# Attention and 64 experts on one core: the order of a product's seven steps with P7 ahead of P3, two places for ys, another place for the second expert's w2, and the first two experts alone

## The chip, the core and the metric

The kernel runs on one core of a Trainium2 chip. The time is device microseconds of one execution, from start to end on that core; lower is better. The engines have their own instruction streams and meet through semaphores: TensorE (PE in the profile, its weight loads PEld), VectorE (DVE), ScalarE (ACT), GpSimd (POOL) and SyncE (SP). Transfers are started by an instruction on a queue (here SP and POOL) and land later. The execution from which the profile was taken took 2610.53 us; the runs without a profile took 2606.79, 2606.75 and 2600.74, median 2606.75.

## The reference

The input x has 4 batches of 1024 rows and 1024 columns, all in float32. With xn the layer norm of x, the result is x + attention(xn) + experts(xn):

```python
q, v, gate = xn @ Wq, xn @ Wv, silu(xn @ Wg)          # each 4096 x 1024 by 1024 x 1024
states[s] = lam * states[s-1] + v[s]                   # a scan over the rows of a batch
y = layernorm(q * states) * ln_g + ln_b
attention = (y * gate) @ Wo                            # a fourth 1024 x 1024 product

# 64 experts over the 4096 rows: 8 per row (softmax, top 8), the first 128 rows of each expert count
h = silu(xg @ w1[e].T) * (xg @ v1[e].T)                # 128 x 1024 by 1024 x 384, twice
y = h @ w2[e]                                          # 128 x 384 by 384 x 1024
out[row of the slot] += y * weight of the slot
```

(The experts take the rows in the order (row, batch); the kernel gathers them by index.)

## The kernel before, in words

**Products in seven steps.** Each 1024-deep product of the attention (v, q, gate, Wo) is cut into 2 x 2 blocks and made with seven block products in place of eight (Strassen's, in Winograd's form). The function `steps` (L128) is a generator: each `next` issues one of the seven, always 8 matmuls of 128 x 512, and the small work behind it. Three PSUM banks are used: a takes P1 (B11), then P6 (T2), P7 (T3) and P4 (T4) added on top; b takes P2 (B21); c takes P5 (T1), then P3 (B22) on top. ACT copies a after P1, c after P5 and a after P6 into a scratch tile (`copied`, L153 to L156), and DVE adds these to a bank to give c11, c12 and c22 (L167, L176, L179). The last step ends with c21 in bank a, which the function `then` takes. Before the change the steps run P1, P2, P5, P6, P3, P7, P4. P7 reads and writes a, c22's add (L179) must read a after P7 and before P4 adds to it; c12's add (L176) reads c after P3.

`product` (L183) drives seven steps for v, q and gate in the first stage, with the last step of one product put between two steps of the next. The first stage, about 1226 us, goes over the 4 batches: layer norm and turn of x, routing (top 8 per row, first 128 rows per expert), the three products, the scan, the second norm (`find_spread`), and the gated rows written to DRAM.

**The experts.** From about 1226 us the class `Experts` runs the 64 experts with the Wo products in between. Each expert has three parts on PE: `hidden` (L943; the two products with w1 and v as one set of block products with seven in place of eight, its right-hand sums made by DVE in `right_sum`, L928, in place in the weight tiles and in t2, t3, t4; 9.08 us), `turn_hidden` (L999; three transposes into bank D, and ACT's copy to hT) and `output` (L1005; two times six matmuls with w2 into banks D and T, ACT's copy times the slot's weight into ys, L1014, and a scatter of ys with addition into the output, L1015, on GpSimd's queue; 5.2 us on PE).

The list `plan` in `run` says which experts go together, and how many Wo steps are put in: ahead of the group's first turn, between each turn and its output, and behind the group. A usual pair runs hidden, hidden, turn, one step, output, turn, two steps, output, and every other pair has one step behind it. Before, expert 0 is alone, then come the pairs (1, 2) to (61, 62), and 63 is alone. There are 16 units of Wo (`project`, L1034), 112 steps in all. The row half lo of a unit (olo) is added to the output by a DMA on GpSimd's queue when five steps have been issued, the other (ohi) in `then`, after the seventh. All these DMAs add into the same output tensor, and those that might touch the same rows as a scatter wait for it, and it for them.

**Order.** In the expert stage the instructions of PE, DVE and ACT are kept in program order (`in_order`, L86); those on SP and POOL are placed by the scheduler of the framework by their readiness. Places in SBUF are handed out by pools: `scratch` (4 tiles of 2 KB a partition) for ACT's copies and two small tiles of the routing, `line` (5 tiles of 4 KB), `left`, `quarter`, `three` and others.

**Loads.** `load(e, n)` (L830) brings v (n = 1), w1 (n = 0) or w2 (n = 2) of expert e, 1536 KB each, on SP's queue; v and w1 have two places each (by e odd or even), w2 has one place, and is loaded as two halves of columns. v and w1 of expert e + 2 are loaded when `hidden(e)` has been issued, w2 of e + 1 when `output(e)` has. `gather` (L850) brings an expert's 128 rows in four indirect DMAs on POOL (xg) and, in a fifth, the weights of its slots (wt, eight places).

Of the kernel before, what the change touches and what calls it, by code (L numbers as in the profile page):

```python
# [8 lines left out]
F32 = mybir.dt.float32  # L9
# [7 lines left out]
P = 128  # L17
# [24 lines left out]
NSLOT = 7  # L42
NWT = 8

# [60 lines left out]
class Pools:  # L105


    def __init__(self, ctx, tc):
        def pool(name, bufs, space=None):
            kw = {} if space is None else {"space": space}  # L110
            return ctx.enter_context(tc.tile_pool(name=name, bufs=bufs, **kw))

        self.one = pool("one", 1)
        self.three = pool("three", 3)
        self.quarter = pool("quarter", 9)
        self.left = pool("left", 2)
        self.line = pool("line", 5)
        self.scratch = pool("scratch", 4)
        self.small = pool("small", 2)

        self.ps2 = pool("ps2", 2, PSUM)
        self.ps1 = pool("ps1", 1, PSUM)
# [14 lines left out]
def steps(nc, pools, lhs, blocks, c11, c12, c22, then, name, begun=None):  # L137
# [28 lines left out]
    yield  # L166
    nc.vector.tensor_tensor(c11, b, s1, ALU.add)  # L167
    c = pools.bank("c", [P, SH], f"pc_{name}")
    acc(c, 4, "T1", True, True)
    s5 = copied(c, 5)  # L170
    yield
    acc(a, 5, "T2", False, True)
    s2 = copied(a, 2)
    yield
    acc(c, 6, "B22", False, True)
    nc.vector.tensor_tensor(c12, c, s2, ALU.add)  # L176
    yield
    acc(a, 3, "T3", False, True)
    nc.vector.tensor_tensor(c22, a, s5, ALU.add)  # L179
    yield  # L180
# [59 lines left out]
def attn_and_routing(  # L240
# [3 lines left out]
    nc = tc.nc  # L244
    one, line, scratch, small = pools.one, pools.line, pools.scratch, pools.small

# [228 lines left out]
    def scored(b):  # L475
# [4 lines left out]
        for k in reversed(range(KD)):  # L480
            for h in (1, 0):
# [7 lines left out]
                )  # L489
        both = scratch.tile([P, SH], F32, tag="sc", name=f"lgs_{b}")  # L490
        nc.scalar.copy(both, two)
# [9 lines left out]
    def route(b, lg):  # L501
# [5 lines left out]
        nc.vector.tensor_reduce(mx, lg, AX.X, ALU.max)  # L507
        sh = scratch.tile(wide, F32, tag="sc", name=f"sh_{b}")
        nc.vector.tensor_tensor(sh, lg, mx.unsqueeze(2).to_broadcast(wide), ALU.subtract)
# [311 lines left out]
class Experts:  # L821
# [8 lines left out]
    def load(self, e, n):  # L830


        if e >= E:
            return
        pools, (w, k) = self.pools, self.ws[n]
        slot = (n, e % 2) if n < 2 else (0, e % 2 ^ 1) if e == E - 1 else n
        if slot not in self.slots:
            t = (pools.x if e == 0 and n < 2 else pools.y)(f"w{n}_{e}")
            self.slots[slot] = t.rearrange("p a b -> p (a b)")
        t = self.weights[e, n] = self.slots[slot].rearrange("p (k f) -> p k f", k=k)  # L840
        if n == 2:
            from_ = w[e].rearrange("p (k f) -> p k f", k=k)
            for cols in (H0, H1):
                self.nc.sync.dma_start(out=t[:, :, cols], in_=from_[:, :, cols])
            return
        done = self.nc.sync.dma_start(out=self.slots[slot], in_=w[e])
        if (e, n) == (1, 1):
            self.tc.keep_in_program_order(done)

    def gather(self, e):  # L850
# [6 lines left out]
        for r in range(NQ):  # L857
# [5 lines left out]
            )  # L863
        nc.gpsimd.indirect_dma_start(
            out=self.wt[:, e % NWT, :],
            out_offset=None,
            in_=self.wtab,
            in_offset=bass.IndirectOffsetOnAxis(ap=self.idx[:, e : e + 1], axis=0),
        )

    def places(self):
# [9 lines left out]
        )  # L881
        self.p6, self.q = t[:, 2 * n : 2 * n + F], u[:, n : n + F]
        self.s = {0: pools.one.tile([P, 4, KH, TH], F32, tag="cur", name="s")}

    def more_places(self):

        pools = self.pools
        t = pools.line.tile([P, S], F32, tag="line", name="s1")
        self.s[1] = t.rearrange("p (i k c) -> p i k c", i=4, k=KH)
        self.ys = pools.line.tile([P, D], F32, tag="line", name="ys")  # L890
        t, u = (pools.scratch.tile([P, SH], F32, tag="sc", name=n) for n in ("act1", "up"))
        self.acts[1], self.up = t[:, 0:F], u[:, 0:F]

# [111 lines left out]
    def output(self, e):  # L1005
        nc, ys, hT = self.nc, self.ys, self.hT
        w2, wt = self.weights.pop((e, 2)), self.wt[:, e % NWT, e : e + 1]
        for h, cols in enumerate((H0, H1)):
# [11 lines left out]
            compute_op=ALU.add,  # L1020
        )


# [10 lines left out]
    def project(self, u, t):  # L1034
# [5 lines left out]

        def add(o, h):
            r0 = b * S + h * SH + m * P
            nc.gpsimd.dma_start(out=self.out[r0 : r0 + P, :], in_=o, accum_op=ALU.add)

        def then(c21):
            nc.scalar.copy(hi[:, H0], c21)
            add(hi, 1)

        for n, _ in enumerate(
            steps(nc, pools, t, self.wo_b, lo[:, H0], lo[:, H1], hi[:, H1], then, f"o_{u}")  # L1050
        ):
            if n == 4:
                add(lo, 0)
            yield

    def begin(self, idx, part):
        self.idx, self.part = idx, part
        v = self.pools.line.tile([P, S], F32, tag="line", name="act")
        self.acts = {0: v[:, 0:F]}
        self.hT = v[:, F : 2 * F].rearrange("p (j i) -> p j i", i=P)  # L1060
        self.wt = self.pools.small.tile([P, NWT, E], F32, tag="sel", bufs=1, name="wt")
        for n in (1, 0):
# [10 lines left out]
    def run(self):  # L1073
# [14 lines left out]

        last = E - 1
        plan = [((0,), 2, (1,), 0), ((1, 2), 0, (1, 2), 1)]  # L1090
        plan += [((e, e + 1), 0, (1, 2), e // 2 % 2) for e in range(3, last - 4, 2)]
        plan += [((e, e + 1), 0, (1, 1), 0) for e in (last - 4, last - 2)]
        plan += [((last,), 1, (0,), 0)]
        todo, u, left = None, 0, 0
# [12 lines left out]
        with in_order(self.tc, ORDERED):  # L1107
# [4 lines left out]
            self.more_places()  # L1112
            for group, ahead, between, behind in plan:
                new = group[-1] + 1
                for e in group:
                    self.hidden(e, e + 2 if e else 1, e != group[-1])
                    for n in (1, 0):
                        self.load(e + 2, n)
                    if e == last - 1:
                        self.load(last, 2)  # L1120
                    if e == group[0]:
                        self.gather(e + 4 if e else 3)
                project(ahead)
                for i, e in enumerate(group):
                    self.turn_hidden(e)
                    project(between[i])
                    if i == 0:
                        if e == 0:
                            for _ in wo_sums:
                                pass  # L1130
                            self.turned(2)
                        for n in (0, 1):
                            self.left_sums(new + n)
                        for n in (3, 1):
                            self.right_sum(new, n)
                    self.output(e)
                    if e + 1 < last:
                        self.load(e + 1, 2)
                    if i == 0:
                        self.gather(group[-1] + 4)  # L1140
                    if e == group[-1]:
                        for n in (2, 4):
                            self.right_sum(new, n)
# [51 lines left out]
```

## Time and profile before

| | before |
|---|---|
| median of 3 runs | 2606.75 us (2600.74 to 2606.79) |
| profiled execution, its time | 2610.53 us |
| its span | 2608.6 us |
| mean granted TensorE clock | 0.998 |
| first stage (0 to 1226 us) | PE busy 1218.06, DVE 796.30, DMA share 0.46 |
| expert stage (1226 to 2592 us) | PE busy 1332.03, DVE 908.82, ACT 366.06, POOL 508.60, DMA share 0.89 |
| HBM read, written | 483.67 MB, 124.81 MB |
| DMA packets | 164338, 593.25 MB |

A line of the waits reads: engine, operation's tile and its line, what it waited for, then us in total, times and longest. A line of the timeline reads: start and duration in us, engine, line, instruction, out<-in, tile and operand shapes, the count of instructions in the row, and in brackets the idle time before it and what ended that. The line numbers are those of the code above. The tail from 2592 us on holds the last two steps of the last Wo unit, the scatter of expert 63 and the last olo and ohi.

### The profile page before, as it was taken

What the parts mean: (1) busy time and instruction counts of PE and PEld (TensorE: products, weight loads), DVE (VectorE), ACT (ScalarE), POOL (GpSimd) and SP (SyncE); (2) the same over time, 40 slices, a digit from 0 to 9 for tenths busy, and PEclk for the clock granted to TensorE, in tenths of its full rate; (3) what the DMA queues carried; (4) which work ended last, traced back from release to release, by engine and by line L of the source; (5) the groups of instructions that cost most, each with busy time, mean ns of one, the idle gap of its engine ahead of it and who ended that gap; (6) DMA issues with size and microseconds to landing.
All of it is one profiled execution on the core that took longest, in us unless ns stands there. A gap on an engine that the chain in (4) does not pass through costs nothing. (4 is left out here: it accounts for less than half of the span.)

```text
span 2608.6 us, 23232 instructions
## 1 busy us (share of the span) xinstructions
PE 2557.6 (98%) x8453; PEld 1129.9 (43%) x8453; DVE 1705.8 (65%) x2116; ACT 612.7 (23%) x1048; POOL 777.6 (30%) x630
## 2 busy tenths in 40 slices
PE   9999999999999999999999999999999999999998
PEld 5444444444444444444444444444444444444443
DVE  7946686384954677266775767575767666666663
ACT  4113112131112211121222223222222222222322
POOL 1452302111021111222343434342434243334321
PEclk9999999999999999999999999999999999999999
DMA  5655625453245441336898988898889889898995
GB/s 188 252 185 207 188 93 165 181 152 119 106 136 214 146 144 67 139 105 231 290 320 281 309 284 311 285 329 269 294 295 319 291 284 300 291 295 289 309 296 138
DMA packets 164338, 593.25 MB, mean 227 GB/s; under 512 B 16880, under 2 KB 53744, under 8 KB 139392
## 3 DMA queue, kind: packets, MB, share of 16 engines
q1 hardware_dynamic: 123472, 448.04, 47.4%
q0 software_dynamic: 40320, 143.72, 20.9%
q8 instruction: 67, 1.10, 0.2%
q14 instruction: 47, 0.39, 0.0%
q10 hardware_dynamic: 432, 0.01, 0.0%
HBM read 483.67 MB, written 124.81 MB: 233 GB/s over the span
## 5 line engine op out<-in xcount | busy, mean ns | idle before, releaser
L940 DVE TENSOR_TENSOR t<-w 128x1536 f32<-128x1536 f32 x128 | 224.0, 1750 | 288.3 <-PE hC L958 285.5
L858 POOL DMA_INDIRECT xg<-rows,tables x256 | 308.0, 1203 | 298.7 <-DVE xgT L901 224.9
L1015 POOL DMA_INDIRECT out_dram<-ys,tables x64 | 117.5, 1836 | 434.7 <-ACT ys L1014 179.2
L144 PE MATMUL pa_g<-xT,w 128*128 128x512 f32 x512 | 230.8, 593 | 0.0
L144 PE MATMUL pa_q<-xT,w 128*128 128x512 f32 x480 | 216.6, 593 | 4.0 <-DVE y L179 4.0
L144 PE MATMUL pa_v<-xT,w 128*128 128x512 f32 x480 | 215.8, 592 | 0.0
L144 PE MATMUL pa_o<-wo_T,gated 128*128 128x512 f32 x384 | 174.2, 596 | 11.8 <-DVE ohi L179 11.8
L1011 PE MATMUL hT<-w,act 128*128 128x512 f32 x384 | 176.0, 594 | 6.3 <-DMA w<-in_w_dram 6.2
L958 PE MATMUL hC<-t,s 128*64 128x384 f32 x512 | 177.5, 489 | 2.5 <-DVE t L940 2.4
L958 PE MATMUL hC<-w,s 128*64 128x384 f32 x512 | 177.5, 490 | 0.0
L1011 PE MATMUL hD<-w,act 128*128 128x512 f32 x384 | 175.3, 592 | 0.6 <-ACT act L1003 0.6
L958 PE MATMUL hB<-w,xgT 128*64 128x384 f32 x512 | 175.7, 486 | 0.0
L958 PE MATMUL hD<-t,s 128*64 128x384 f32 x512 | 175.7, 486 | 0.0
L958 PE MATMUL hA<-w,s 128*64 128x384 f32 x512 | 175.6, 486 | 0.0
L958 PE MATMUL hA<-w,xgT 128*64 128x384 f32 x512 | 175.6, 486 | 0.0
L144 PEld LDWEIGHTS pa_g<-xT,w 128*128 128x128 f32 x512 | 96.8, 190 | 122.7 <-issue 121.8
L692 POOL DMA_DIRECT2D gated<-y x64 | 48.5, 763 | 320.3 <-DVE y L687 309.4
L144 PEld LDWEIGHTS pa_q<-xT,w 128*128 128x128 f32 x480 | 90.5, 190 | 117.0 <-issue 109.8
L144 PEld LDWEIGHTS pa_v<-xT,w 128*128 128x128 f32 x480 | 91.1, 190 | 115.0 <-issue 110.0
L1011 PEld LDWEIGHTS hT<-w,act 128*128 128x128 f32 x384 | 72.4, 190 | 100.5 <-issue 87.3
L144 PE MATMUL pc_g<-xT,w 128*128 128x512 f32 x256 | 115.7, 592 | 0.0
L144 PE MATMUL pc_q<-xT,w 128*128 128x512 f32 x256 | 115.5, 593 | 0.0
(244 smaller groups left out, 4350.8 us busy)
## 6 DMA issues: line engine op xcount, KB each, us to landing
w<-in_v_dram SPq DMA_DIRECT2D x64, 1536.0 KB
w<-in_w_dram SPq DMA_DIRECT2D x64, 1536.0 KB
w<-in_w_dram SPq DMA_DIRECT2D x128, 768.0 KB
w<-wsum SPq DMA_DIRECT2D x36, 1792.0 KB
wsum<-w POOLq DMA_DIRECT2D x12, 1792.0 KB
x<-in_x_dram SPq DMA_DIRECT2D x32, 512.0 KB
rows<-x POOLq DMA_DIRECT2D x32, 512.0 KB
gated<-y POOLq DMA_DIRECT2D x64, 256.0 KB
```

The source lines that it names most:

```text
L144: nc.tensor.matmul(ps, lhsT=lhs[:, slot, k, :], rhs=blocks[right][:, k, :], start=start and k == 0, stop=stop and k == KH - 1, skip_group_ ...
L692: nc.gpsimd.dma_start(out=gated[b, :, :, slot, m, :].rearrange("u p j -> p u j"), in_=yc[:, h * SH : (h + 1) * SH].rearrange("p (u j) -> p ...
L858: nc.gpsimd.indirect_dma_start(out=self.xg[:, e % 2 * NQ + r, :], out_offset=None, in_=self.rows.rearrange("n (q c) -> (n q) c", q=NQ), in ...
L940: self.nc.vector.tensor_tensor(to, a, b, ALU.subtract)
L958: nc.tensor.matmul(bank[half], lhsT=a[:, ks[k], :], rhs=b[:, ks[k], :], start=(k == 0), stop=(k == len(ks) - 1), tile_position=(0, half.st ...
L1011: nc.tensor.matmul(ps, lhsT=hT[:, j, :], rhs=w2[:, j, cols], start=(j == 0), stop=(j == KF - 1))
L1015: nc.gpsimd.indirect_dma_start(out=self.out, out_offset=bass.IndirectOffsetOnAxis(ap=self.idx[:, e : e + 1], axis=0), in_=ys, in_offset=No ...
```

## The change

- **Steps.** P6 comes third, P5 fourth, P7 fifth, P3 sixth, P4 seventh. The add of c22 (DVE) follows P7, that of c12 follows P3. In `project` olo is added to the output one step later (after P3, which completes c12). Of the last unit alone, ohi goes out as two halves: the columns of c22 after P7, those of c21 at the end.
- **Places.** The scratch pool has 2 tiles, not 4, and the line pool 6, not 5. The two small routing tiles (lgs, sh) move from scratch to line. There are two ys tiles, used by e odd or even. The act tile of the line pool holds both `acts` and wt, which has 4 places and not 8; hT takes the place of p6; `up` takes the small tile where wt was.
- **Loads.** w2 of any expert is one DMA of 1536 KB. The second expert of a pair has its w2 loaded into the place of its own w1 once its `hidden` has been issued; w1 of the next second expert goes, after the first expert's `output`, into the place where the first expert's w2 was. w2 of the next first expert is loaded after the group's last output. v of both, and w1 of the next first expert, are loaded after `hidden` as before. wt of expert e + 4 is gathered right behind the scatter of e.
- **Groups.** Experts 0 and 1 go alone, then come the pairs (2, 3) to (62, 63); two steps lie ahead of expert 0's turn, one between its turn and output, one ahead of expert 1's turn. The steps before the last two of unit 15 are as many as before, 110. The sums of Wo's blocks are finished after the steps ahead of expert 0's turn, and xg is turned for both experts of the next group where a group of one comes before a pair.

The diff, cut to its core:

```diff
 class Pools:
-        self.line = pool("line", 5)
-        self.scratch = pool("scratch", 4)
+        self.line = pool("line", 6)
+        self.scratch = pool("scratch", 2)
...
 def steps(...):
     nc.vector.tensor_tensor(c11, b, s1, ALU.add)
+    acc(a, 5, "T2", False, True)
+    s2 = copied(a, 2)
+    yield
     c = pools.bank("c", [P, SH], f"pc_{name}")
     acc(c, 4, "T1", True, True)
     s5 = copied(c, 5)
     yield
-    acc(a, 5, "T2", False, True)
-    s2 = copied(a, 2)
+    acc(a, 3, "T3", False, True)
+    nc.vector.tensor_tensor(c22, a, s5, ALU.add)
     yield
     acc(c, 6, "B22", False, True)
     nc.vector.tensor_tensor(c12, c, s2, ALU.add)
-    yield
-    acc(a, 3, "T3", False, True)
-    nc.vector.tensor_tensor(c22, a, s5, ALU.add)
     yield
     acc(a, 2, "T4", False, True)
...
 def load(self, e, n):
-        slot = (n, e % 2) if n < 2 else (0, e % 2 ^ 1) if e == E - 1 else n
+        pair, second = max(e - 2, 0) // 2, e % 2
+        if n == 1 or n == 0 and not second:
+            slot = n, second
+        elif n == 0:
+            slot = pair % 2
+        else:
+            slot = 1 if e < 2 else (pair + 1 - second) % 2
...
-        if n == 2:
-            from_ = w[e].rearrange("p (k f) -> p k f", k=k)
-            for cols in (H0, H1):
-                self.nc.sync.dma_start(out=t[:, :, cols], in_=from_[:, :, cols])
-            return
-        done = self.nc.sync.dma_start(out=self.slots[slot], in_=w[e])
+        done = self.nc.sync.dma_start(out=t, in_=w[e])
...
 def places(self):
+        self.hT = self.p6.rearrange("p (j i) -> p j i", i=P)
 def more_places(self):
-        self.ys = pools.line.tile([P, D], F32, tag="line", name="ys")
+        self.ys = [pools.line.tile([P, D], F32, tag="line", name=f"ys{i}") for i in range(2)]
 def output(self, e):
-        nc, ys, hT = self.nc, self.ys, self.hT
+        nc, ys, hT = self.nc, self.ys[e % 2], self.hT
...                                    # after the scatter
+        self.gather_wt(e + NWT)
 def project(self, u, t):
+        parts = u == B * NM - 1
         def then(c21):
             nc.scalar.copy(hi[:, H0], c21)
-            add(hi, 1)
+            add(hi, 1, H0 if parts else slice(0, D))
...
-            if n == 4:
+            if n == 4 and parts:
+                add(hi, 1, H1)
+            if n == 5:
                 add(lo, 0)
 def run(self):
-        plan = [((0,), 2, (1,), 0), ((1, 2), 0, (1, 2), 1)]
-        plan += [((e, e + 1), 0, (1, 2), e // 2 % 2) for e in range(3, last - 4, 2)]
-        plan += [((e, e + 1), 0, (1, 1), 0) for e in (last - 4, last - 2)]
-        plan += [((last,), 1, (0,), 0)]
+        plan = [((0,), 2, (1,), 0), ((1,), 1, (0,), 0)]
+        plan += [((e, e + 1), 0, (1, 2), int(e % 4 == 0)) for e in range(2, E - 4, 2)]
+        plan += [((E - 4, E - 3), 0, (1, 2), 0), ((E - 2, E - 1), 0, (1, 1), 0)]
...
+                    self.load(e + 2, 1)                       # after hidden(e)
+                    if i == 0:
+                        self.load(e + 2, 0)
+                    else:
+                        self.load(e, 2)
...
+                    if i == 0 and len(group) > 1:             # after output(e)
+                        self.load(new + 1, 0)
...
+                    if e == group[-1]:
+                        self.load(new, 2)
```

## The prediction

> **What bounds the kernel now.** I read the busy shares first, then TensorE's waits, then the timeline around each kind of wait, then the windows of the two stages. The busy shares (busy us, share of the span, instructions) say which engine's time is the time of the kernel:
>
> ```profile
> PE 2557.6 (98%) x8453; PEld 1129.9 (43%) x8453; DVE 1705.8 (65%) x2116; ACT 612.7 (23%) x1048; POOL 777.6 (30%) x630
> ```
>
> TensorE is idle for 51 of 2608.6 us. The change takes no matmul away, so all that it can win lies in the waits of PE (us in total, times, longest):
>
> ```profile
> PE hD L1002 <- ACT ys L1014: 12.0, 5, 3.3
> PE pa_o L144 <- DVE ohi L179: 11.8, 15, 0.8
> PE hT L1011 <- DMA w<-in_w_dram: 6.2, 5, 2.6
> PE pa_q L144 <- DVE y L179: 4.0, 3, 2.0
> PE hC L958 <- DVE t L940: 2.4, 1, 2.4
> ...
> PE hD L1002 <- issue: 1.6, 1, 1.6
> ...
> PE hD L1011 <- ACT act L1003: 0.6, 1, 0.6
> ```
>
> Each row has its place in the code. The second is the last two steps of a Wo product side by side: the DVE must read bank a for ohi before P4 may add to it. On PE's timeline (start, duration; idle before):
>
> ```profile
> 1713.60 3.60 PE L144 MATMUL pa_o<-wo_T,gated 128*128 128x512 f32 x8
> 1717.98 3.70 PE L144 MATMUL pa_o<-wo_T,gated 128*128 128x512 f32 x8 [0.78 <-DVE ohi L179]
> 1721.52 2.74 PE L1011 MATMUL hD<-w,act 128*128 128x512 f32 x6
> ```
>
> From 1713.60 to 1721.52 the pair of steps takes 7.92 us. Undisturbed steps start 3.44 and 3.43 us apart; the third kind of wait, on the second expert's w2, follows them:
>
> ```profile
> 1754.27 3.60 PE L144 MATMUL pb_o<-wo_B,gated 128*128 128x512 f32 x8
> 1757.71 3.60 PE L144 MATMUL pc_o<-wo_B,gated 128*128 128x512 f32 x8
> 1761.14 2.74 PE L1011 MATMUL hD<-w,act 128*128 128x512 f32 x6
> 1766.52 2.84 PE L1011 MATMUL hT<-w,act 128*128 128x512 f32 x6 [2.64 <-DMA w<-in_w_dram]
> ```
>
> The first row is the single ys: ACT may not empty the output banks into ys before the last scatter has read it, and the next turn needs bank D. The wait itself, and what the 8 matmuls behind it cost:
>
> ```profile
> ACT ys L1014 <- DMA out_dram<-ys,tables: 170.7, 31, 9.1
> ```
> ```profile
> 2270.26 0.77 PE L1002 MATMUL hD<-ident,act 128*128 128x128 f32 x3 [3.26 <-ACT ys L1014]
> 2270.82 5.11 PE L144 MATMUL pb_o<-wo_B,gated 128*128 128x512 f32 x8
> ```
>
> ACT stands there once a pair, 5.5 us on the mean; only some of it reaches PE. GpSimd's queue shows why the scatter comes late, in the pair in which a product ends: olo, scatter, ohi and scatter, each after the one before has landed.
>
> ```profile
> 1712.61 1.01 POOL L1043 DMA_DIRECT2D out_dram<-olo  x1
> ...
> 1722.15 1.61 POOL L1015 DMA_INDIRECT out_dram<-ys,tables  x1 [8.53 <-DMA out_dram<-olo]
> ...
> 1730.93 0.95 POOL L1043 DMA_DIRECT2D out_dram<-ohi  x1 [5.86 <-DMA out_dram<-ys,tables]
> 1739.47 1.59 POOL L1015 DMA_INDIRECT out_dram<-ys,tables  x1 [7.58 <-issue]
> ```
>
> The expert stage as a window (length; busy us of PE, PEld, DVE, ACT, POOL; clock; DMA share; GB/s):
>
> ```profile
> 1226.00:2592.00 1366.00, 1332.03 (x5434) 583.19 (x5433) 908.82 (x1133) 366.06 (x704) 508.60 (x398) 1.00 0.89 292
> ```
>
> DVE has a third of it free; DMA at 0.89 is the resource to fear.
>
> **The change part by part.** The sum is made against the profiled execution, 2610.5 us (span 2608.6), which lies 3.8 us above the median of 2606.75. A measurement of this kernel can tell about 0.3%, 8 us.
>
> *Order of the steps.* P2, P6, P5, P7, P3, P4: all 56 matmuls stay. Between P7 and P4 lies P3, 3.44 us, against the 0.78 that DVE was late. Fourteen such pairs (the fifteenth lies in the tail) at 7.92 − 6.87 = 1.05 give **14.7**. In the attention the row on y is the same adjacency in the q product: 4.0 idle and 0.2 of restart each, **4.6**; the longest wait, 2.0, is under the new gap of 3.44. What comes late instead: c12 is finished a step later and its add sits right before P4, but P4 writes bank a, and bank c is wanted only by the next product. P6 ahead of P5 makes T2 wanted one step sooner; in the experts gated's sums are long done by then. The olo DMA on GpSimd goes out one step later.
>
> *Scratch 4 to 2.* Three copies pass through two buffers: s2's copy waits for c11's add of s1, and s5's for none that is open. The trace shows no wait for scratch. Below: 0; above: three products of each of 4 batches late by some 0.1 us, about 1. I take 0 and keep 1. Lower than zero is excluded: no wait of before is on scratch.
>
> *Two ys.* ACT's copy now waits for the scatter of two experts before. Counted from the pair's start, the first expert's scatter goes out at about 28 us and its place is wanted again at 64; scatters land 6.1 to 14.3 us after issue (median 8.0). Five waits 12.0, the one put down to "issue" 1.6, 0.2 restart each: **14.8**. With them go the slow matmuls after the two waits of 3.26 and 2.76: 8 in 5.11 and 5.30 instead of 3.60, **3.2**. The Trainium skill ("TensorE: Matmul & The Clock Gate", Part 1: The HAM clock gate) has the clock halved only after an idle window of about 3.4 us; no wait here is so long, and by that rule this term would be 0 and the result 3 us higher. The trace differs: 3.26 and 2.76 lost the clock, while 3.02 and 2.64 did not.
>
> *GpSimd's order.* In the pair with a product's end it becomes scatter, wt, olo, ohi, scatter; olo and ohi touch different rows and wait only for the first scatter. That is three landings in a row, not four. The wt gather for e+4 stands behind the scatter of e and is used some 80 us later, against a slowest landing of 12.6: nothing.
>
> *Loads.* w2 of the second expert starts when its own hidden part has read w1, about 17 us into the cycle of 39.6, and is wanted 17.4 us later. One DMA of 1536 KB replaces two halves; SP is busy 0.33 for it, not twice 0.55. Landings of 1536 KB take 7.2 to 13.8 us (w1, median 9.7): five waits of 6.2 and 0.2 each, **7.2**. In exchange w1 of the next second expert goes out only when the first output has read w2. Its first DVE use is about 15 us later and PE needs the result after 21; the slowest landing leaves 1.3 us. v on SP stays in front of both. w2 of the next first expert has 22 us. Neither costs anything while no landing exceeds 15; DVE standing on that load would hold the adds of the hidden part behind it, so its price beyond 19 us is one for one on PE, 31 times.
>
> The Trainium skill ("DMA: Bandwidth & Descriptors", Issuing engines are not separate DMA queues) says that transfers of all issuing engines share the same 16 engines: moving loads then buys no room, only other times. By the row, 0.89 of 1366 is 1216 us of transfers, 0.92 of a stage 41 us shorter; it would not bind, though landings may lengthen.
>
> *Alone at the start, a pair at the end.* The 2.4 wait at 1258 (hC on the DVE's sums, 2.6 with restart) goes, as expert 1 does not come straight behind expert 0's output. New are T2's Wo sum, by the DVE's order about 1.0 late now that P6 is third, and expert 1 with one step ahead of its turn: the last expert, built so now, has 0.57 and restart, so I take 1.1. Net **0.5**; ends 0 and 2.6. The last expert in a pair loses its 0.57: **0.7**.
>
> *Tail.* After the last scatter followed ohi, 5.5 us to land. Now olo and half of ohi go beside each other and the other half at the very end: −1.5 to +0.5. I take −1, set against the 1 of scratch.
>
> Sum: 14.7 + 14.8 + 3.2 + 7.2 + 4.6 + 0.5 + 0.7 = **45.7**, and 2610.5 − 45.7 = **2565** us. The spread of the runs shown (2601 to 2607) is of the size of these waits, so I don't carry the 3.8 over.
>
> **The rivals.**
>
> *Weights stay a wait.* For it: DMA share 0.89, rising to 0.92, and four loads of 1536 KB (v and w1, v and w2) within some 10 us of each cycle. Against it: the page's slices reach 329 GB/s and the new stage needs 399 MB in 1325 us, 301. If w2's 7.2 stays and as much to four times as much comes from late w1, the time is 2580 to 2600.
>
> *The scatters still hold ys.* If the three landings together with the gathers ahead of them on GpSimd outlast 49 us, the ys and clock terms (18.0) stay: 2583. Against it: from the first scatter to the landing of the second I count 27 to 31 us (out at 28, landed at 55 to 59), and the second's place is wanted again at 77.
>
> *Slower: w1 of the second expert.* It alone starts later than before (at 27 us of the cycle, not 17). Each landing beyond 19 us is paid 31 times; 45.7 / 31 = 1.5, so at 20.5 us on the mean the gain is gone, and at 22 the time is 2655. For it: nothing but the crowding; the slowest of before was 13.8.
>
> *No change.* If PE's waits were only the visible part of a bound on DMA, each that goes would return elsewhere, within 8 us of 2607. Against it: w2 alone is waited for, and 5 times in 64.
>
> **How the numbers follow.** The forecast (2557 to 2575: tail and start at their ends, runs 3.8 under the profile) has 0.72; weights 0.12; scatters 0.06; no change 0.03; slower 0.07. The low end, 2556, takes the tail's and the median's share; the high end, 2592, holds the scatters and most of the weights. Faster 0.90, same 0.03, slower 0.07.
>
> **What would show it.** The waits of PE without the rows on ohi and y, and ACT's on its scatter gone: those steps are right. A row of PE on ys: the scatter rival. DVE L940 waiting on w from DRAM, or hC on t: w1 is late, and I am wrong. A row hT on w: w2 is not early enough. The attention up to 1226 should be about 4.6 shorter, the expert stage about 41.

## The result and the profile after

| | before | changed |
|---|---|---|
| median | 2605.74 us (2600.74 to 2606.79, 4 runs) | 2570.29 us (2569.67 to 2570.74, 4 runs) |
| ratio, 95% interval | | 0.9868 [0.985, 0.9885] |
| span of the profiled execution | 2608.6 us | 2567.9 us |
| mean granted TensorE clock | 0.998 | 0.999 |
| expert stage as a window (1226 to 2592 us; 1226 to 2551 us) | DMA share 0.89, 292 GB/s | 0.90, 301 GB/s |

The changed kernel is 35 us faster, against 2565 forecast (of the span 40.7 went, of 45.7 in the sum). The busy shares and PE's waits of the changed kernel:

```profile
PE 2545.3 (99%) x8453; PEld 1130.9 (44%) x8453; DVE 1691.7 (66%) x2116; ACT 615.2 (24%) x1048; POOL 799.7 (31%) x631
```
```profile
PE sT L537 <- DVE sel L516: 5.2, 4, 1.4
...
PE pa_v L144 <- ACT sc_v L155: 1.3, 1, 1.3
PE pa_o L144 <- DVE wo_T L71: 0.9, 1, 0.9
PE hD L1020 <- ACT t L1012: 0.6, 1, 0.6
```

The rows on ohi, y, ys and w2 are gone, and ACT's row on its scatter with them. The first two rows here lie in the attention: the one on sel has grown (before: 1.1 in one wait), the one on sc_v is new. The last two are the start with expert 1 alone. PE's timeline where a product ends, for the pair of steps that stood side by side:

```profile
1717.95 3.60 PE L144 MATMUL pc_o<-wo_B,gated 128*128 128x512 f32 x8
1721.39 3.60 PE L144 MATMUL pa_o<-wo_T,gated 128*128 128x512 f32 x8
1724.82 2.74 PE L1020 MATMUL hD<-w,t 128*128 128x512 f32 x6
```

P3 and P4 take 6.87 us together, without a gap. GpSimd's queue around it, now scatter, olo, ohi, scatter, where olo and ohi go out 0.64 us apart:

```profile
1718.79 2.71 POOL L1024 DMA_INDIRECT out_dram<-ys,tables  x1 [1.76 <-ACT ys L1023]
...
1728.02 0.96 POOL L1053 DMA_DIRECT2D out_dram<-olo  x1 [5.24 <-issue]
1728.66 1.27 POOL L1053 DMA_DIRECT2D out_dram<-ohi  x1
...
1742.56 1.77 POOL L1024 DMA_INDIRECT out_dram<-ys,tables  x1 [12.63 <-DMA out_dram<-ohi]
```

Three marks of PE's timeline split each span: the start of the last matmul of a gate product, the start of the last matmul of an output, and the end.

| profiled execution | attention: to the last gate matmul | experts: from there to the last output matmul | tail |
|---|---|---|---|
| before | 1231.7 | 1360.0 | 16.9 |
| changed | 1231.0 | 1318.4 | 18.5 |
| difference | −0.7 | −41.6 | +1.6 |
| forecast | −3.6 (y 4.6, scratch +1) | −41.1 | −1 |

So the experts came out within half a microsecond of the forecast, and the attention and the tail missed. Whether the terms inside the 41.1 were right, only runs that take the parts apart can tell.

### The profile page after: what moved, and what is told of

Its sections match the earlier page's. It is cut to its first block, busy times and chain, and to the rows that moved or that the text cites. A ratio compares the mean times of both kernels' runs of the same rounds, so it can differ in the third digit from the quotient of the medians.

```text
span 2567.9 us, 23154 instructions
## 1 busy us (share of the span) xinstructions
PE 2545.3 (99%) x8453; PEld 1130.9 (44%) x8453; DVE 1691.7 (66%) x2116; ACT 615.2 (24%) x1048; POOL 799.7 (31%) x631
## 2 busy tenths in 40 slices
DMA packets 122497, 593.24 MB, mean 231 GB/s; under 512 B 15872, under 2 KB 52736, under 8 KB 89360
## 4 chain that ended last, share of the span: by engine, by line
PE 95%; DVE 3%; DMA 1%; issue 0%; ACT 0%; POOLq 0%; POOL 0%; DVEq 0%
PE pa_g L144 8%; PE pa_o L144 8%; PE pa_v L144 8%; PE pa_q L144 8%; PE hC L967 7%; PE hA L967 6%; PE hD L1020 6%; PE hT L1020 6%; PE hD L967 6%; PE pc_g L144 4%; PE pc_o L144 4%; PE pc_q L144 4%; PE pc_v L144 4%; PE hB L967 3%; PE pb_o L144 2%; PE pb_q L144 2%
## 5 line engine op out<-in xcount | busy, mean ns | idle before, releaser
L1024 POOL DMA_INDIRECT out_dram<-ys,tables x64 | 134.9, 2108 | 396.2 <-ACT ys L1023 182.6
L1020 PE MATMUL hD<-w,t 128*128 128x512 f32 x384 | 175.3, 592 | 0.6 <-ACT t L1012 0.6
L1020 PE MATMUL hT<-w,t 128*128 128x512 f32 x384 | 175.2, 592 | 0.0
L144 PE MATMUL pc_o<-wo_B,gated 128*128 128x512 f32 x256 | 115.2, 593 | 0.0
```

Of the source, the lines that this page charges most:

```text
L144: nc.tensor.matmul(ps, lhsT=lhs[:, slot, k, :], rhs=blocks[right][:, k, :], start=start and k == 0, stop=stop and k == KH - 1, skip_group_ ...
L1020: nc.tensor.matmul(ps, lhsT=hT[:, j, :], rhs=w2[:, j, cols], start=(j == 0), stop=(j == KF - 1))
L1024: nc.gpsimd.indirect_dma_start(out=self.out, out_offset=bass.IndirectOffsetOnAxis(ap=self.idx[:, e : e + 1], axis=0), in_=ys, in_offset=No ...
```

## The experiments

Two theories stood at the start. The first is the sum itself: each part is worth what its own rows in the waits of before were worth (steps 19.3, ys and clock 18.0, loads 7.2). The rival: some of these waits stand in for each other, so that the parts are worth other amounts. Medians of kernels run at different times are compared to about 2 us, since the kernel before had medians from 2605.7 to 2609.5 in the four sets of runs; the ratios are each to its own set.

### The old order of the steps

```diff
-    acc(a, 5, "T2", False, True)
-    s2 = copied(a, 2)
-    yield
     c = pools.bank("c", [P, SH], f"pc_{name}")
     acc(c, 4, "T1", True, True)
     s5 = copied(c, 5)
     yield
-    acc(a, 3, "T3", False, True)
-    nc.vector.tensor_tensor(c22, a, s5, ALU.add)
+    acc(a, 5, "T2", False, True)
+    s2 = copied(a, 2)
     yield
     acc(c, 6, "B22", False, True)
     nc.vector.tensor_tensor(c12, c, s2, ALU.add)
     yield
+    acc(a, 3, "T3", False, True)
+    nc.vector.tensor_tensor(c22, a, s5, ALU.add)
+    yield
     acc(a, 2, "T4", False, True)
...
-            if n == 4 and parts:
+            if n == 5 and parts:
                 add(hi, 1, H1)
```

> The changed kernel with the seven steps in the old order (P5, P6, P3, P7, P4); two places of ys, loads, groups and pools stay as changed; olo goes out at the same step, the half of ohi of the last unit one step later. In the changed kernel's profile the four waits of PE on sel in the attention (5.2 us) are new. Theory A (the smaller pools make the routing late, not the order of the steps): the stalls between P7 and P4 come back, 15 in the experts and tail at 1.05 = 15.7, those on y in the attention about 4, and the waits on sel stay or grow: 2570 + 19 to 24, 2589 to 2594. Theory B (P7 one step earlier on the DVE makes the routing late): the waits on sel go back to 1.1 while the stalls come back: 2570 + 15.7 + 4 - 5, about 2585. Rival C (the order of the steps won nothing, since the scatters or the loads take the time): within 8 us of 2570.

Measured: 2583.6 us (2583.2 to 2583.9), ratio 0.9905 [0.9885, 0.9926]. PE's waits:

```profile
PE pa_o L144 <- DVE ohi L179: 12.5, 16, 0.8
PE pa_q L144 <- DVE y L179: 3.6, 3, 1.6
...
PE sT L537 <- DVE sel L516: 0.7, 3, 0.2
```

The order is worth 13.3, not 19.3. The stalls of the experts came back in full (1331.8 against 1318.4 between the marks), those on y too, but the waits on sel nearly left. Theory B has the number: in the attention the new order wins 4 and pays about as much for sel. It doesn't have the reason. The routing is no earlier on the DVE with the old order: its first subtraction (L509) starts at 351.70 in this run, at 349.44 in the changed kernel and at 339.88 before. It is late in both kernels with the new pools, and only where PE asks for sel differs.

### One place for ys

```diff
-        self.ys = [pools.line.tile([P, D], F32, tag="line", name=f"ys{i}") for i in range(2)]
+        self.ys = [pools.line.tile([P, D], F32, tag="line", name="ys")] * 2
```

> The changed kernel with one place for ys, all else as changed. Theory A (the prediction's sum): ACT waits for the last scatter again, six waits of PE or so on ys, 14.8, and two of them lose the clock, 3.2: 2570 + 18 = 2588, with a row of PE on ACT ys in the waits. Since the chain on GpSimd is one landing shorter than before, it may be less, down to 2575. Rival (the second place is not what took the waits away, but the shorter chain olo and ohi side by side): 2570 to 2573 and no row on ys.

Measured: 2573.6 us (2571.8 to 2574.6), ratio 0.9866 [0.9845, 0.9887]. PE's row on ys is small, and ACT's own wait for the scatter has shrunk from 170.7 us, 9.1 at the longest, with the same single place, to the two rows below:

```profile
PE hD L1011 <- ACT ys L1023: 2.8, 2, 1.5
```
```profile
ACT ys L1023 <- DMA act<-wtab,tables: 53.3, 15, 5.2
ACT ys L1023 <- DMA out_dram<-ys,tables: 43.7, 15, 6.1
```

The second row of ACT names the gather of wt, which goes out right behind the scatter. Yet in these waits, too, the scatter of the last expert landed just before ACT went on (mostly 0.1 to 0.4 us), so ACT's wait for it is the sum, 97.0 us. So the second place is worth 3.3 us, not the 18.0 that I gave it; that is nearer to the rival, though a small row on ys is there. Something else in the change took the ys waits away.

### One ys, and the room given back to the attention

```diff
-        self.line = pool("line", 6)
-        self.scratch = pool("scratch", 2)
+        self.line = pool("line", 5)
+        self.scratch = pool("scratch", 4)
...
-        both = line.tile([P, SH], F32, tag="line", name=f"lgs_{b}")
+        both = pools.scratch.tile([P, SH], F32, tag="sc", name=f"lgs_{b}")
...
-        sh = line.tile(wide, F32, tag="line", name=f"sh_{b}")
+        sh = pools.scratch.tile(wide, F32, tag="sc", name=f"sh_{b}")
...
-        self.ys = [pools.line.tile([P, D], F32, tag="line", name=f"ys{i}") for i in range(2)]
+        self.ys = [pools.line.tile([P, D], F32, tag="line", name="ys")] * 2
```

> As the run with one place of ys, and the room that this frees given back to the attention as before: four scratch tiles, lgs and sh of the routing in scratch, five line tiles. It differs from that run in nothing else. Theory A (pools make the routing late): the waits on sel go from 5.2 to about 1.1, with the scratch wait of 1.3: 5 to 6 us under the run with one ys. Theory B (the order of the steps makes it late): equal to it within 1 us.

Measured: 2581.0 us, with runs from 2573.8 to 2586.7 (0.9903 [0.9875, 0.993]). There is no row on sel any more; in its place stands

```profile
PE pa_v L144 <- ACT sc_v L155: 10.7, 4, 2.7
```

Both theories fail. The old places do end the waits on sel, but with lgs and sh in scratch again and the new order of the steps a copy in the v product comes late in each batch, and the attention ends at 1235.0, later than in either kernel. PE's and ACT's timeline in the second batch show which copy:

```profile
397.36 2.84 PE L144 MATMUL pa_v<-xT,w 128*128 128x512 f32 x6 [2.74 <-ACT sc_v L155]
```
```profile
395.77 1.06 ACT L633 ACTIVATE sum<-away 128x1024 f32<-128x1024 f32 x1 [14.26 <-DVE away L632]
396.74 0.57 ACT L155 COPY sc_v<-pa_v 128x512 f32<-128x512 f32 x1
```

PE waits ahead of P7, which adds to bank a and needs ACT's copy of a after P6. On ACT's queue this copy stands behind an operation of the second norm (L633), which waits for the DVE. Before, L633 started at 395.45, and P7 at 397.43 without a wait; with the new order P7 is due a step sooner, and the norm's operation is not.

The experts take 1318.4 us here between the marks, as long as with two places of ys. Only the shortest of the four runs was profiled. Why they spread over 13 us is open; the two longest show a granted clock of 0.996, the shortest 0.998.

### The old loads

```diff
-        pair, second = max(e - 2, 0) // 2, e % 2
...
+        slot = (n, e % 2) if n < 2 else n
...
+        if n == 2:
+            from_ = w[e].rearrange("p (k f) -> p k f", k=k)
+            for cols in (H0, H1):
+                self.nc.sync.dma_start(out=self.weights[e, n][:, :, cols], in_=from_[:, :, cols])
+            return
...
-                    if i == 0:
-                        self.load(e + 2, 0)
-                    else:
-                        self.load(e, 2)
+                    self.load(e + 2, 0)
...
-                    if i == 0 and len(group) > 1:
-                        self.load(new + 1, 0)
...
+                    self.load(e + 1, 2)
                     if e == group[-1]:
-                        self.load(new, 2)
```

> The changed kernel with the loads of before: one place for w2, in two halves after the output of the expert before, w1 of the second expert after its own hidden part. Theory A (the prediction's sum): PE waits on w2 again, five or six times, 7.2 in all: 2577, and since the stage is shorter by 41 us, and PE comes to w2 without a stall ahead of it, up to twice that, 2585. Rival (the merged load or the crowding of DMA decides, not the place): within 3 us of 2570, without a row of hT on w.

Measured: 2602.5 us (2595.6 to 2604.4, 10 runs), ratio 0.9969 [0.9955, 0.9983].

```profile
PE hT L1019 <- DMA w<-in_w_dram: 17.1, 12, 1.6
PE hD L1019 <- DMA w<-in_w_dram: 5.2, 3, 3.6
```

Taken back from the changed kernel the loads are worth 32 us, and everything else together, without them, 0.3% of the time. Both theories had less: 7 to 15 us, or nothing. The row on w2 was 6.2 us before the change; with ys and step stalls gone the two rows are 22.3, and PE's busy time is 8.0 longer than in the changed kernel (2553.3 against 2545.3). The wait comes once in each two pairs, every 84 us, at the second output of the pair without a product's end. In the kernel before, this pair held mostly a wait on ys, at its second turn, or a wait on w2, some 10 us later at its second output, never both.

### The place of w2 or its single DMA

The first of two kernels leaves the changed kernel's places and brings w2 in halves:

```diff
+        if n == 2:
+            from_ = w[e].rearrange("p (k f) -> p k f", k=k)
+            for cols in (H0, H1):
+                self.nc.sync.dma_start(out=self.weights[e, n][:, :, cols], in_=from_[:, :, cols])
+            return
         done = self.nc.sync.dma_start(out=t, in_=w[e])
```

The second has the old loads, as in the experiment before, but w2 in one DMA:

```diff
+        slot = (n, e % 2) if n < 2 else n
...
-                    if i == 0:
-                        self.load(e + 2, 0)
-                    else:
-                        self.load(e, 2)
+                    self.load(e + 2, 0)
...
-                    if i == 0 and len(group) > 1:
-                        self.load(new + 1, 0)
...
+                    self.load(e + 1, 2)
                     if e == group[-1]:
-                        self.load(new, 2)
```

> The changed kernel with every w2 in two DMAs of 768 KB in place of one of 1536 KB, at the changed kernel's places and times of issue. With the loads of before the changed kernel took 32 us more (2602.5); this run asks whether the place or the single DMA is worth that. Theory A (the place: w2 of the second expert starts 10 us earlier in the cycle): within 3 us of 2570, no row of hT on w. Theory B (the single DMA, with its longer packets, moves the bytes in less time): 2580 to 2600, with hT on w or DVE t on w.

> The loads of before (one place for w2, filled after the output of the expert before; w1 of the second expert after its own hidden part), but w2 in one DMA of 1536 KB. Theory A (place): 2602 or more. The one DMA goes out when the last columns of the first output are read and its first columns are wanted 7.2 us later; whole loads land 7.2 to 13.8 us after issue, median 9.7, so 2.5 us late in each of 31 pairs, some 78 us: 2648 (2602 to 2700), with the row on hD, not hT. Theory B (single DMA is what wins): 2570 to 2585.

Measured: 2570.8 us (2570.4 to 2571.1; 0.985 [0.9824, 0.9875]) for the halves at the new place, 2617.0 us (2607.4 to 2626.4; 1.0031 [1.0012, 1.005]) for the one DMA at the old place, whose first output half now waits:

```profile
PE hD L1014 <- DMA w<-in_w_dram: 32.9, 18, 3.7
```

The place, with the time of issue that goes with it, is worth all of it. The number of packets (164482 with halves, 122497 without) made no difference to the time.

### w1 late, the prediction's slower rival

```diff
-            slot = pair % 2
+            slot = 0
         else:
-            slot = 1 if e < 2 else (pair + 1 - second) % 2
+            slot = 0 if second and e > 1 else 1
...
                     if i == 0 and len(group) > 1:
-                        self.load(new + 1, 0)
+                        self.load(new, 2)
...
                     if e == group[-1]:
-                        self.load(new, 2)
+                        if len(group) > 1:
+                            self.load(new + 1, 0)
+                        else:
+                            self.load(new, 2)
```

> The changed kernel with two loads exchanged: w2 of the next first expert goes out after the first output, w1 of the next second expert only after the second output, 12.4 us later than in the change. This is the prediction's rival that ends slower, made on purpose: it prices a w1 that lands after DVE wants it. By the prediction's count the load is wanted 15 us (first use on DVE) to 19 us (PE) after the first output's end, so 3 to 7 us after its new issue; landings of 1536 KB take 7.2 to 13.8 us, median 9.7. Theory A (paid one for one on PE beyond 19): 3 us in each of 30 pairs, 2660 (2600 to 2760), with DVE t on w from DRAM and hC or hA on DVE t. Rival (the DVE has slack enough): 2570 to 2580.

Measured: 2664.9 us (2660.2 to 2668.6), ratio 1.0205 [1.0174, 1.0235]. The chain is the one forecast: DVE stands on the load with the hidden part's adds behind it, and PE on those. From DVE's and PE's waits:

```profile
DVE w L949 <- DMA w<-in_w_dram: 107.0, 16, 8.9
```
```profile
PE hC L967 <- DVE t L987: 68.9, 16, 6.5
```

It is paid in 16 waits and not in each of the 30 pairs, at 4.3 us of waiting each. These 69 us are not all: the clock falls to 0.987, and PE's busy time grows by 29.0 us (2574.3 against 2545.3), which is the rest of the 98 us by which the span is longer than the changed kernel's.

### Old steps and one ys together

The steps as in the first experiment, and with them

```diff
-            if n == 4 and parts:
+            if n == 5 and parts:
                 add(hi, 1, H1)
...
-        self.ys = [pools.line.tile([P, D], F32, tag="line", name=f"ys{i}") for i in range(2)]
+        self.ys = [pools.line.tile([P, D], F32, tag="line", name="ys")] * 2
```

> The changed kernel with the old order of the steps and one ys; loads, groups and pools as changed. Alone the old order cost 13.3 and the one ys 3.3. Theory A (they add): 2587. Theory B (a stall between P7 and P4 gives the scatter its time, so one ys costs nothing beside it): 2583 to 2584.5. Theory C (before, the ys waits of 18 came with the order of the steps, through the DMAs of olo and ohi): 2595 or more.

Measured: 2586.0 us (2583.6 to 2588.7), ratio 0.9911 [0.9885, 0.9937]. Theories A and B lie within the spread of the runs; theory C is out. In the profile PE has no row on ys at all, and ACT waits for the scatter 53.0 us in all (17.3 put down to it, 35.7 to the gather of wt behind it). So the ys waits of before did not come with the order of the steps. Against the kernel before, what is left of the change here is the loads, the groups, the pools and olo's later DMA, and that alone is worth some 23 us.

### The steps alone, on the kernel before

The seven steps as the changed kernel has them, and with them

```diff
-            if n == 4:
+            if n == 5:
                 add(lo, 0)
...
                 project(ahead)
+                if group[0] == 0:
+                    for _ in wo_sums:
+                        pass
...
-                            for _ in wo_sums:
-                                pass
```

> The kernel before with the new order of the steps alone (P6, P5, P7, P3, P4; olo after P3, and the Wo sums finished a step earlier at expert 0, as the new order needs them); loads, ys, groups and pools as before. Theory A (each part is worth by itself what its waits were): 15.7 in experts and tail and 4 in the attention, 20 less than before, 2587. Theory B (with the old loads PE only comes sooner to a w2 that lands no sooner): the stalls on ohi go and the rows of hT on w and hD on ys grow by nearly as much; the gain is that of the attention and a little more, 3 to 7 us.

Measured: 2605.8 us (2601.6 to 2611.7, 10 runs), ratio 0.9996 [0.9981, 1.0011]: nothing that can be told. PE's and ACT's waits:

```profile
PE hT L1011 <- DMA w<-in_w_dram: 17.3, 12, 1.6
PE pa_v L144 <- ACT sc_v L155: 9.8, 4, 2.7
PE hD L1011 <- DMA w<-in_w_dram: 6.4, 3, 4.3
```
```profile
ACT ys L1014 <- DMA out_dram<-ys,tables: 74.5, 27, 5.4
```

The row on ohi is gone, and the row on ys with it, although ys has one place; its queue on GpSimd now has olo and ohi side by side behind the first scatter, as in the changed kernel. But ys and w2 together were 14.8 + 7.2 = 22 before (restarts included), and w2 alone is 23.7 of idle time now. The two waits are one shortage: where ys held PE back, w2 had the time to land. That is theory B for the experts, though in the two profiled executions they are still 8.5 us shorter between the marks (1351.5 against 1360.0). The gain that theory B left to the attention did not come: it is 2.8 us longer (1234.5), by the row on sc_v, which is that of the run with the old places.

### sh beside lgs

```diff
-    sels = {}
+    sels, shs = {}, {}
...
-        both = line.tile([P, SH], F32, tag="line", name=f"lgs_{b}")
+        both = line.tile([P, S], F32, tag="line", name=f"lgs_{b}")
+        shs[b] = both[:, H1].rearrange("p (n e) -> p n e", e=E)
+        both = both[:, H0]
...
-        sh = line.tile(wide, F32, tag="line", name=f"sh_{b}")
+        sh = shs.pop(b)
```

> The changed kernel with sh of the routing in the second half of the line tile of lgs, in place of a line tile of its own. The scheduler then puts the first operation of the routing (L509) ahead of the add of c22 on the DVE's queue, as it stood before the change. Theory A (the four waits on sel, 5.2 us, come from that place in the queue): they go back to 1 or less, 4 us less, 2566. Theory B (the DVE has too much to do at that point with P7 one step earlier, wherever sh lies): as much waits elsewhere in the attention (y, scratch, sel), 2569 to 2571.

What it goes after is seen on DVE's timeline of the changed kernel. The routing's first subtraction (L509) stands behind the add of c22 of the v product, which waits for PE, and PE later for sel:

```profile
348.84 0.69 DVE L176 TENSOR_TENSOR hi<-pa_v,sc_v 128x512 f32<-128x512 f32 x1 [8.46 <-PE pa_v L144]
349.44 0.68 DVE L509 TENSOR_TENSOR sh<-lg,mx 128x512 f32<-128x512 f32 x1
```
```profile
356.96 0.60 PE L537 MATMUL sT<-ident,sel 128*64 128x128 f32 x4 [1.37 <-DVE sel L516]
```

In the kernel before, L509 ran ahead of the adds that end the v product:

```profile
339.88 0.68 DVE L509 TENSOR_TENSOR sh<-lg,mx 128x512 f32<-128x512 f32 x1
```

Measured: 2567.8 us (2567.1 to 2568.9), ratio 0.9846 [0.9832, 0.986], 2.5 us under the changed kernel. The row on sel is gone, but

```profile
PE pa_v L144 <- ACT sc_v L155: 2.6, 2, 1.9
```

took 1.3 us of it, with 0.6 on sc_q beside it. The attention ends at 1228.4, 2.6 us sooner. Theory A, with a part of B.

### ohi of the last unit whole

```diff
-        parts = u == B * NM - 1
+        parts = False
```

> The changed kernel with ohi of the last unit in one DMA after the last step, not in two halves. In the changed kernel's profile the last scatter waits 3.85 us for the first half to land, though ys was ready about 1.8 us before. Theory A (the half stands in the chain of the tail): 1.5 to 2 us less, 2568.5. Theory B (the half at the end lands as much sooner as it costs): 2570 to 2571.

Measured: 2569.6 us (2569.1 to 2570.5), ratio 0.9852 [0.9836, 0.9869]; no difference that can be told. The tail on GpSimd in the changed kernel:

```profile
2548.43 0.92 POOL L1053 DMA_DIRECT2D out_dram<-ohi  x1 [4.79 <-issue]
2553.20 1.61 POOL L1024 DMA_INDIRECT out_dram<-ys,tables  x1 [3.85 <-DMA out_dram<-ohi]
2559.68 0.92 POOL L1053 DMA_DIRECT2D out_dram<-olo  x1 [4.87 <-DMA out_dram<-ys,tables]
2561.11 0.89 POOL L1053 DMA_DIRECT2D out_dram<-ohi  x1 [0.51 <-issue]
```

Whole, the last scatter goes out 2.6 us sooner (2550.63), but the whole ohi beside olo takes 8.9 us to land, the half 5.1. Theory B.

### Together, with the last steps ahead of the last output

The edits of the last two experiments, and in the plan

```diff
-        plan += [((E - 4, E - 3), 0, (1, 2), 0), ((E - 2, E - 1), 0, (1, 1), 0)]
+        plan += [((E - 4, E - 3), 0, (1, 2), 0), ((E - 2, E - 1), 0, (1, 3), 0)]
```

> The changed kernel with sh beside lgs, ohi whole, and the last two steps of Wo ahead of the last output (one step before the first and three before the second output of the last pair), so that olo and ohi land while the last output is made and only the last scatter follows. Theory A: 4 less in the attention, 3 less in the tail (the end then follows the last output by one scatter): 2563. If the attention gives nothing: 2567. Rival (the last scatter has to wait for ohi and comes later than in the change): 2570 or more.

Measured: 2565.9 us (2565.6 to 2566.7), ratio 0.9839 [0.9825, 0.9852], the fastest of all, 4.3 us under the changed kernel in medians of different sets. GpSimd's queue at the end:

```profile
2547.66 0.93 POOL L1055 DMA_DIRECT2D out_dram<-olo  x1 [5.67 <-DVE olo L179]
2550.99 0.88 POOL L1055 DMA_DIRECT2D out_dram<-ohi  x1 [2.40 <-ACT ohi L1060]
2556.87 1.61 POOL L1026 DMA_INDIRECT out_dram<-ys,tables  x1 [5.00 <-DMA out_dram<-ohi]
```

olo and ohi land while the last output is made, and one scatter follows. From the start of the last matmul to the end it is 10.1 us, not 11.6. Some 1.8 us of the gain are the attention's. The time lies between theory A (2563) and the case without a gain in the attention (2567).

## Why the prediction was right, and where not

**The total** was 5 us too good, inside the range. The shortfall has two places: the attention (−0.7, not −3.6) and the tail (+1.6, not −1).

**What bounds the kernel**: right. DMA did not become the bound; the forecast of 301 GB/s and 0.92 for the shorter stage is 301 and 0.90.

**Order of the steps, 14.7 + 4.6.** The mechanism held: the rows on ohi and y went, and between the marks of the experts the old order costs 13.4. The term for the attention failed: the waits on y were replaced by waits on sel and sc_v. Two steps are at fault. One is "*Scratch 4 to 2* … I take 0": I looked for a wait on a scratch tile, and the move of sh to another pool changed the order on the DVE's queue instead, 9.6 us later for L509. The old order and the other place of sh each end the waits on sel. The other is "What comes late instead", which names c12 and T2 and not ACT's copy of a after P6, wanted by P7 a step sooner. With sh in its old place that costs 9.8 to 10.7 us on sc_v, and the attention ends at 1234.5 to 1235.0; so the order alone loses in the attention. With sh beside lgs it ends at 1228.4, 3.4 us sooner than before, and most of the 4.6 is there.

**Two ys, 14.8 + 3.2.** The waits went, but not by the second place: it is worth 3.3 at most, and nothing with the old order (1331.8 us of experts with one place and with two). The step that failed is the attribution. The row named a scatter that landed late, and the text had the reason beside it, four landings in a row on GpSimd's queue, but gave the three in a row of the new order no price. With olo after the first scatter and one ys, ACT's wait for the scatter is 74.5 with the old loads, 97.0 with the new ones and 53.0 with the new loads and the old order, not 170.7, and PE's row on ys is 2.8 or none. What these runs share and the kernel before lacks is olo's later DMA (and the Wo sums finished sooner, once, at the start), which points to it. No run moved olo's DMA alone, so its share is not measured by itself; that the second place is not what did it, is.

**Loads, 7.2.** The largest miss inside the sum: 32 us when taken back from the changed kernel. The row of before was small because ys and w2 were late in the same pair, and PE can wait only once: without the ys waits, and with the old loads, w2's rows are 22.3 and 23.7. The counted window was right (landings of the second w2: 8.8 to 14.3 us, of 17.4), and so was the new window of w1 (7.0 to 10.7, of 15).

These two errors cancel in large part: 18.0 + 7.2 = 25.2 is the sum of both rows, and the change removes both. That the experts came out within 0.5 us is luck, and no evidence for the terms: taken back one by one between the marks, the order is worth 13.4, the second ys 3.3 and the loads 29.8.

**The slower rival** had the right place: with w1 12.4 us later the kernel is 2% slower than before. Its price of one for one, 31 times, is not what was paid: 16 waits, 69 us, and 29 us of slower matmuls, which it did not count. (Its own figure at 22 us should be 2565 + 31 × 3 = 2658, not 2655.) **The scatters still hold ys** and **weights stay a wait** did not happen in the changed kernel, but the second is what the parts without the loads give (2602 to 2606). **No change** is what the steps alone gave, and in part as named there: the wait returned elsewhere, on w2. But no bound on DMA sent it there, since with the other times of issue the same bytes cost PE no wait, and another part was lost in the attention.

**Start and last expert**: 0.9 on wo_T and 0.6 on the turn of expert 1 stand for the 1.0 and 1.1 forecast. **Tail**: the half of ohi was put between the last two scatters, and the last one waited 3.85 us for it; I had priced the two DMAs at the end and not this place in the queue. Without the half (ohi whole) the tail is no shorter, though: 19.6 between the last marks. Either way olo, a step later than before, no longer lands ahead of the last scatter (it went out at 2587.05 before, the scatter at 2593.34) but at the very end beside ohi.

## What to carry to other kernels

Waits close together in a cycle do not add up: the one that comes first gives the next its time, and the one that it hides comes out when it is gone. Sum such rows as one term, and ask which part of the change removes the last of them, since without it the others may bring little (here the steps alone: 0.9996, a part of it lost in the attention). When a tile moves to another pool, compare the order of the engine queues and not only the waits for that pool. And where a wait is put down to one of two DMAs that land together, as ACT's on the gather of wt, add the rows.

## What the runs showed of the hardware

- Whether a wait of PE loses the clock is not decided by its length between 1.9 and 3.2 us. In the run with w2 in one DMA at the old place, six matmuls after a wait of 2.58 took 4.36 us (2.81 where the clock was kept), after one of 2.86 they took 2.81, after one of 3.16 4.32:

```profile
1438.24 4.32 PE L1014 MATMUL hD<-w,t 128*128 128x512 f32 x6 [3.16 <-DMA w<-in_w_dram]
...
1526.03 2.81 PE L1014 MATMUL hD<-w,t 128*128 128x512 f32 x6 [2.86 <-DMA w<-in_w_dram]
...
2122.37 4.36 PE L1014 MATMUL hD<-w,t 128*128 128x512 f32 x6 [2.58 <-DMA w<-in_w_dram]
```

  In the run with the steps alone a wait of 1.94 was enough, with a granted clock of 0.50 over the window 2524.95 to 2528.30; and of its waits of 2.74 on sc_v the one at 395.50 lost the clock, those at 700.38 and 1003.84 did not:

```profile
2524.25 4.51 PE L1011 MATMUL hD<-w,act 128*128 128x512 f32 x6 [1.94 <-DMA w<-in_w_dram]
```

  The Trainium skill ("TensorE: Matmul & The Clock Gate", Part 1: The HAM clock gate) says that the window of about 3.4 us runs freely. If so, the moment decides and not only the length, which agrees with these rows. Its one idle window of about 3.4 us as what it takes to lose the clock does not: 1.94 was enough here.
- In the changed kernel the same 1536 KB from DRAM take 7.0 to 10.7 us (median 7.8) for w1 of the second expert, which goes out 10.3 us behind the load ahead of it, and 8.8 to 14.3 (median 11.7) for w2 of the second expert, which goes out 2.6 and 9 us behind two other loads and beside the gathers of xg. So the moment of issue within the cycle goes with some 4 us of landing. Split into two, this w2 landed later (its second half 10.7 to 17.1 us after issue, median 12.5), still in time: PE had no wait on it, and the kernel's time stayed.
